# Three of seven block products of an output projection made by seven quarter products each, in an attention kernel on one core

## The chip, the cores and the metric

The kernel runs on one core of a Trainium2 chip. The metric is the device time of one execution in microseconds (us). A core has a tensor engine (PE), a vector engine (DVE), a scalar engine (ACT), GpSimd (POOL) and a sync engine (SP), which here issues all data transfers from one queue, in order. Tiles live in SBUF (128 partitions); PE writes its sums to PSUM banks, which DVE and ACT read[...].

## The reference

Two layers run one after the other on x, of shape (8, 512, 32, 32), float32. Each is a group norm (8 groups in the first, 32 in the second), attention with 8 heads of 64 over the 1024 pixels of an image, an output projection, and the residual added:

```python
qkv = jnp.einsum('oc,bcn->bon', qkv_w, xt) + qkv_b[None, :, None]
...
attn = jnp.einsum('bhdi,bhdj->bhij', q, k) * scale
attn = jax.nn.softmax(attn, axis=-1)
out = jnp.einsum('bhij,bhdj->bhdi', attn, v)
out = out.reshape(B, C_, N)
out = jnp.einsum('oc,bcn->bon', proj_w, out) + proj_b[None, :, None]
return out.reshape(B, C_, H, W) + residual
```

## The kernel before

A *unit* is one image in one layer: 16 units u, 0 to 7 in layer 0 and 8 to 15 in layer 1. The program is written out for all of them, and every engine runs its part in program order. Unit u consists of the products q, k and v (`projections`), then the output projection of the unit before (`project(old, ...)`), then attention with 64 steps. So the projection of unit 3 stands in the middle of unit 4. The last unit's projection (`project_last`) stands at the end and is made in another way.

**Seven block products.** q, k, v and the projection are 512x512 by 512x1024 products. `blocks` makes each of them from halves: with the Strassen-Winograd scheme, four result quarters need seven products of half size in place of eight. The left factors are made once per layer from the weights (`mix_weights`), the right ones per unit (`mix_right`). A product by factor k is four matmuls of 128x128 by 512 columns (L352), and each stands in the profile as two records. `blocks` takes the factors in the order 1, 6, 2, 7, 5, 4, 3, in the PSUM banks bx, by, bz, and calls `done` after each. DVE adds the banks to partial sums p1, u2, u3 (`c11`, `others`).

**Quarter products.** For q and k of every unit but the first, three of the seven (`INNER`, factors 2, 4 and 3) are split again (`last_products`): seven products of 128x128 by 256 columns (L370) in place of four matmuls of 512. Parts that don't go straight into the bank go through two scratch banks `one` and `two`, from which ACT copies them to an SBUF tile `rest`; PE writes `one` again only when the copy is done. Then GpSimd adds two quarters of `rest` (L390, L391) and adds `rest` to the result tiles (`rests`, L470). The right factors are made by GpSimd (`mix_inner`), the left ones once per layer (`mix_inner_left`), which then go by way of DRAM.

**The projection** (`project`) makes all seven in full. DVE adds bias and residual (`plus`, L507) and writes the result into the residual tiles w.res, from which each half tile is stored at once by SP (`store`, L528):

```python
w.evac[h] = nc.vector.tensor_add(
    w.res[o][:, ts(h, FD)], bank[:, i, :], more[:, i, :]
)
store(o, h)
```

`others` is called for result quarters (1,1), (1,0) and (0,1) in this order; (1,0) concerns residual tiles 2 and 3, (0,1) tiles 0 and 1.

**Attention.** At step s PE makes scores s (L603) and, two steps later at first, the product with v (L631); ACT makes the exponential between them (L611) and DVE sums it (L648, L650). The exponentials' tiles p are four buffers of `ppool`, the same that w.res had: the first four exponentials write to the buffers in the order in which these come free. `gate` makes PE wait for what has read a bank. Between two chunks of eight steps, `evacuate` copies a bank to a `tmp` tile of `tmppool` and DVE adds to it. `accpool`, `trpool`, `tpool` hold DVE's sums, transposes and the mixed factors.

**GpSimd's other work.** Its queue also has, in unit 7 ahead of the projection of unit 6, the mixing of layer 1's weights:

```python
if u == B - 1:
    lefts, mixing_w = mix_weights(1, load_weights(1), nc.gpsimd)
    for part in mixing_w:
        part()
```

**Order of small work.** `rest` in the main loop lists work by the running number g of `done` calls: 1 to 7 in q, 8 to 14 in k, 15 to 21 in v. At 17, 19 and 20 DVE makes the right factors of the coming projection (L769).

Of the kernel before, what the change touches and what calls it, by code (L numbers as in the profile page):

```python
# [11 lines left out]
F32 = mybir.dt.float32  # L12
# [6 lines left out]
P = 128  # L19
# [13 lines left out]
def fast_path(ctx, tc, x, qkv_wT, proj_wT, vecs, groups, out, flag):  # L33
# [14 lines left out]
    nc = tc.nc  # L48
    B, C, N = x.shape
# [13 lines left out]
    def pool(name, bufs, **kw):  # L63
# [8 lines left out]
    ppool = pool("ppool", 4)  # L72
    accpool = pool("accpool", 2)
    tpool = pool("tpool", 1)
    tmppool = pool("tmppool", 2)
    trpool = pool("trpool", 2)
    rbpool = pool("rbpool", 1)
    small = pool("small", 2)
# [15 lines left out]
    okay = const.tile([P, 2 * BL], F32, name="okay")  # L94
    asum = const.tile([P, 2 * B * CC], F32, name="asum")

    inner_left = [
        mids.tile([P, 2, len(INNER), 3, P], F32, tag=f"il{l}", name=f"il{l}") for l in range(2)
    ]
# [57 lines left out]
    def mix_right(name, low, high):  # L157


        b11, b12 = low[:, :, :FD], low[:, :, FD:]  # L160
        b21, b22 = high[:, :, :FD], high[:, :, FD:]
        t1, t2, t4 = (
            tpool.tile([P, 2, FD], F32, tag=f"{name[0]}{k}", name=f"{name}_t{k}")
            for k in (1, 2, 4)
        )
        sub = nc.vector.tensor_sub
        parts = (
            partial(sub, t1, b12, b11), partial(sub, t2, b22, t1),
            partial(sub, t4, b21, t2), partial(sub, b12, b22, b12),
        )  # L170
        return {1: b11, 2: b21, 3: b22, 4: t4, 5: t1, 6: t2, 7: b12}, parts

    def mix_inner(u, right):

# [16 lines left out]
    def inner_lefts(k, left, made):  # L191
        a11, a12 = left[:, 0, :P], left[:, 1, :P]
        a21, a22 = left[:, 0, P:], left[:, 1, P:]
        s1, s2, s4 = (made[:, i, :] for i in range(3))
        return {1: a11, 2: a12, 3: s4, 4: a22, 5: s1, 6: s2, 7: a21}

    def mix_inner_left(l, lefts):


        add, sub = nc.gpsimd.tensor_add, nc.gpsimd.tensor_sub  # L200

        def part(n, k):
            t = tpool.tile([P, 2, FD], F32, tag=("o1", "o2", "o4")[n], name=f"l{k}_{l}")
            t = t.rearrange("p a b -> p (a b)")[:, : 6 * P].rearrange("p (i s o) -> p i s o", i=2, s=3)
            for i in range(2):
                left = lefts[i][k]
# [7 lines left out]
                nc.sync.dma_start(inner_left[l][:, i, n], t[:, i])  # L214

        return [partial(part, n, k) for n, k in enumerate(INNER)]

    def load_inner_left(u):

        l, _ = units[u]  # L220
        flat = vpool.tile([P, NT, C], F32, tag="v", name=f"il_{u}").rearrange("p t o -> p (t o)")
        n = len(INNER) * 3 * P
        made = []
        for i in range(2):
            part = flat[:, i * n : (i + 1) * n].rearrange("p (k s o) -> p k s o", s=3, o=P)
            nc.sync.dma_start(part, inner_left[l][:, i])
            made.append({k: part[:, j] for j, k in enumerate(INNER)})
        return made, flat[:, NT * C - 2 * FD :].rearrange("p (a b) -> p a b", a=2)

    def load_proj(l, tag):  # L230
# [100 lines left out]
    class Unit:  # L331
        pass

    def blocks(name, left, right, tokens, c11, others, done, u3, inner=None, rests=None):

        bx, by, bz = apair[0], sbank[0], apair[1]
        sums = []  # L340

        def products(bank, k, start, stop):
            a, b = left[k], right[k]
# [14 lines left out]
        def last_products(bank, k, one, two):  # L358


            if inner is None:
                products(bank, k, False, True)
                return None
            left, right = inner[k]
            one, two = one[:, 0, :FD2], two[:, 0, :FD2]
            tag = ("o1", "o2", "o4")[INNER.index(k)]
            rest = tpool.tile([P, 2, FD], F32, tag=tag, name=f"m{k}_{name}")

            def product(j, dst, start, stop):
                nc.tensor.matmul(  # L370
                    dst, left[j], right[j], start=start, stop=stop, skip_group_check=True
                )
# [8 lines left out]
            nc.scalar.copy(rest[:, 1, FD2:], two)  # L381
            product(4, bank[:, 1, :FD2], False, True)
            product(7, one, False, True)
            nc.scalar.copy(rest[:, 1, :FD2], one)
            return rest

        def add_rest(r, h, rest):
# [37 lines left out]
        others(0, 1, bz, u2)  # L425
        add_rest(0, 1, rest)
        done(sums)

    def projections(w, rest):

# [12 lines left out]
        for sel, bias in (("q", QB), ("k", KB)):  # L443
# [30 lines left out]
            if w.inner:  # L474
# [4 lines left out]
            blocks(f"{sel}_{u}", left, w.right, False, c11, others, done, u3, inner, rests)  # L479
            setattr(w, sel, tiles)  # L480

        w.v = vpool.tile([P, NT, C], F32, tag="v", name=f"v_{u}")
# [16 lines left out]
    def project(w, after):  # L499
# [30 lines left out]
        def c11(bank):  # L530
            for i in range(2):
                cols = w.res[i][:, :FD]
                plus(cols, i, bank[:, i, :], cols)
                store(i, 0)

        def others(r, h, bank, more):
            for i in range(2):
                o = 2 * r + i
                w.evac[h] = nc.vector.tensor_add(  # L539
                    w.res[o][:, ts(h, FD)], bank[:, i, :], more[:, i, :]  # L540
                )
                store(o, h)

        w.evac = [None, None]
        blocks(f"o_{w.u}", w.left, w.right_o, False, c11, others, done, (rbpool, "rb"))

    def project_last(w, rest):

# [24 lines left out]
    def attention(w, at_step, at_end):  # L573
# [6 lines left out]
        n_chunks = CC * NH  # L580
        n_steps = n_chunks * NT
        state = {"exp": [], "p": [], "free": [[], []], "acc": {}}

        def scores(s):
            c, t = divmod(s, NT)
# [30 lines left out]
        def products(s):  # L616
            p = state["p"][s]
            c, t = divmod(s, NT)
            pr, qh = divmod(c, NH)
            banks = abank[2 * (c % 2) : 2 * (c % 2) + 2]  # L620
            before = [state["exp"][s]]
            if t == 0:
                before += state["free"][c % 2]
            if s == 0:
                before += w.last["v"] + w.evac_before
            gate(*before)
            for r in range(2):
                rows = slice(r * H, (r + 1) * H)
                for j in range(2):
                    lo = pr * P + j * D  # L630
                    nc.tensor.matmul(  # L631
                        banks[r][j * H : (j + 1) * H, :],
                        w.v[rows, t, lo : lo + D],
                        p[rows, j, :],
                        start=(t == 0),
                        stop=(t == NT - 1),
                    )
# [14 lines left out]
        def evacuate(c):  # L652
            pr, qh = divmod(c, NH)
            banks = abank[2 * (c % 2) : 2 * (c % 2) + 2]
            tmp = tmppool.tile([P, FD], F32, tag="tmp", name=f"tmp_{u}_{c}")
            i0 = nc.scalar.copy(tmp, banks[0])  # L656
            i1 = nc.vector.tensor_add(w.ao[pr // 2][:, pr % 2, ts(qh, FD)], banks[1], tmp)  # L657
            state["free"][c % 2] = [i0, i1]
# [100 lines left out]
            for h in range(NH):  # L759
                add_bias(CC - 1, h)  # L760

        mixing = []

        def mix(*which):
            if not mixing:
                w.right_o, parts = mix_right(f"o_{u}", *w.ao)
                mixing.extend(parts)
            for i in which:
                mixing[i]()  # L769

        return {
            4: [lambda: reciprocals(CC - 1)], 10: [divide_last],
            17: [partial(mix, 0, 1)], 19: [partial(mix, 2)], 20: [partial(mix, 3)],
        }


    xn = load_xn(0)
# [15 lines left out]
    for u in range(2 * B):  # L793
        w = Unit()
        w.u, w.right, w.lefts, w.inner = u, right, lefts, None
        w.evac_before = []

        rest.setdefault(2, []).extend([mixing[3], mixing[2]])
        if u > 0:
# [3 lines left out]
                part()  # L803
            rest[2].extend(parts[-4:])
        if u == B + 1:
            rest[16] = mixing_o
        projections(w, rest)
        if old is not None:
            old.res = load_res(old.u)
# [10 lines left out]
        if u == B - 1:  # L820
            lefts, mixing_w = mix_weights(1, load_weights(1), nc.gpsimd)
            for part in mixing_w:
                part()
        left_parts = mix_inner_left(units[u + 1][0], lefts) if u in (0, B - 1) else ()

        def stats_of(*which):
            for i in which if nxt is not None else ():
# [324 lines left out]
```

## Time and profile before

| | |
|---|---|
| Three runs | 3311.31, 3311.65, 3310.22 us; median 3311.31 |
| Profiled execution | 3310.82 us, span 3308.9 us from first to last instruction, granted PE clock 1.0 |
| Busy | PE 99%, PE's weight loads 52%, DVE 74%, ACT 46%, POOL 19% |
| PE matmuls by line | attention L631 1098.8 us and L603 1056.9 us plus 50.8 us |
| Projection's block products, L352 on o_t and ao | each group of 120 records 53.9 us |
| Store of a half residual tile, L528 | 256 KB, 2.1 us from issue to landing |

In the profile a row names a line of the kernel, an engine, an operation and the tiles (written <- read). "Busy" is the union of the durations of a group. Matmuls are pipelined, so two that follow each other overlap in the timeline; the distance between their starts tells what one costs. In brackets stands how long the engine was idle before, and what ended that. SPq and ACTq are the queues of the engines. A span can be compared with the runs' times only after the small difference between them.

### The profile page before, as it was taken

What the parts mean: (1) busy time and instruction counts of PE and PEld (TensorE: products, weight loads), DVE (VectorE), ACT (ScalarE), POOL (GpSimd) and SP (SyncE); (2) the same over time, 40 slices, a digit from 0 to 9 for tenths busy, and PEclk for the clock granted to TensorE, in tenths of its full rate; (3) what the DMA queues carried; (4) which work ended last, traced back from release to release, by engine and by line L of the source; (5) the groups of instructions that cost most, each with busy time, mean ns of one, the idle gap of its engine ahead of it and who ended that gap; (6) DMA issues with size and microseconds to landing.
All of it is one profiled execution on the core that took longest, in us unless ns stands there. A gap on an engine that the chain in (4) does not pass through costs nothing.

```text
span 3308.9 us, 53663 instructions
## 1 busy us (share of the span) xinstructions
PE 3281.0 (99%) x21542; PEld 1736.5 (52%) x21542; DVE 2435.9 (74%) x2977; ACT 1525.1 (46%) x1909; POOL 616.7 (19%) x620
## 2 busy tenths in 40 slices
PE   8999999999999999999999999999999999999999
PEld 4445464554645546455464644646456464554633
DVE  4876958769587695867958679586795967859577
ACT  1552726527164361743617436273462734527244
POOL 0231030300304013044220401204021040210400
PEclk9999999999999999999999999999999999999999
DMA  2111020111101112012120111201112011120111
GB/s 78 43 46 71 23 77 27 47 65 36 66 29 51 58 36 77 21 48 96 50 84 27 48 58 36 83 15 47 65 36 77 15 53 58 36 77 15 60 65 47
DMA packets 72906, 169.48 MB, mean 51 GB/s; under 512 B 21456, under 2 KB 23248, under 8 KB 72656
## 3 DMA queue, kind: packets, MB, share of 16 engines
q1 hardware_dynamic: 72656, 166.01, 15.1%
q8 instruction: 174, 2.85, 0.4%
q14 instruction: 76, 0.62, 0.1%
HBM read 127.95 MB, written 36.44 MB: 50 GB/s over the span
## 4 chain that ended last, share of the span: by engine, by line
PE 99%; DVE 1%; DMA 0%; issue 0%; ACT 0%; POOL 0%; SPq 0%; ACTq 0%
PE a L631 26%; PE s L603 25%; PE a L352 20%; PE s L352 16%; PE a L370 4%; PE s L370 4%; PE a L603 1%; PE s L554 0%; PE a L554 0%; DMA xn<-x_dram 0%; DVE x L539 0%; DVE stats L247 0%; PE a L259 0%; ACT p L611 0%; DVE acc L648 0%
## 5 line engine op out<-in xcount | busy, mean ns | idle before, releaser
L611 ACT ACTIVATE p<-s 128x1024 f32<-128x1024 f32 x976 | 996.9, 1023 | 819.5 <-PE s L603 785.2
L631 PE MATMUL a<-p,v 64*64 64x512 f32 x8192 | 1098.8, 589 | 2.3 <-ACT p L611 2.3
L603 PE MATMUL s<-q,k 64*64 64x512 f32 x7808 | 1056.9, 590 | 1.4 <-DVE v L492 1.4
L650 DVE TENSOR_TENSOR acc<-acc,p 128x1024 f32<-128x1024 f32 x768 | 952.2, 1240 | 90.4 <-ACT p L611 42.2
L631 PEld LDWEIGHTS a<-p,v 64*64 64x64 f32 x8192 | 382.1, 131 | 499.6 <-ACT p L611 352.1
L603 PEld LDWEIGHTS s<-q,k 64*64 64x64 f32 x7808 | 380.9, 133 | 442.0 <-issue 439.5
L803 POOL TENSOR_TENSOR r<-xn 128x256 f32<-128x256 f32 x60 | 75.0, 1250 | 1166.7 <-DVE acc L650 1049.4
L279 POOL TENSOR_TENSOR y<-var,half 128x4 f32<-128x4 f32 x16 | 32.2, 2014 | 1052.0 <-DVE var L277 1052.0
L648 DVE TENSOR_TENSOR acc<-p,p 128x1024 f32<-128x1024 f32 x128 | 153.9, 1203 | 12.0 <-ACT p L611 11.9
L663 DVE STREAM_TRANSPOSE tr<-acc 128x1024 f32<-128x1024 f32 x128 | 157.9, 1234 | 0.0
L673 DVE TENSOR_REDUCE red<-tr 128x32 f32<-128x1024 f32 x128 | 153.9, 1202 | 0.6
L657 DVE TENSOR_TENSOR ao<-a,tmp 128x512 f32<-128x512 f32 x128 | 87.9, 687 | 68.2 <-ACT tmp L656 68.1
L352 PE MATMUL a<-xn,w 128*128 128x512 f32 x272 | 125.6, 605 | 4.0 <-DVE xn L307 4.0
L400 ACT COPY p_o<-a 128x1024 f32<-128x1024 f32 x15 | 15.2, 1012 | 244.2 <-PE a L352 244.2
L352 PE MATMUL s<-xn,w 128*128 128x512 f32 x256 | 115.2, 593 | 1.6 <-DVE xn L441 1.6
L352 PE MATMUL a<-w,xn 128*128 128x256 f32 x512 | 115.7, 379 | 0.0
L352 PE MATMUL a<-x_t,s1w 128*128 128x512 f32 x256 | 115.1, 592 | 0.0
L352 PE MATMUL s<-x_t,s2w 128*128 128x512 f32 x256 | 115.1, 592 | 0.0
L470 POOL TENSOR_TENSOR k<-k,m_k 128x512 f32<-128x512 f32 x90 | 112.2, 1268 | 0.0
L470 POOL TENSOR_TENSOR q<-q,m_q 128x512 f32<-128x512 f32 x90 | 112.0, 1265 | 0.0
L352 PE MATMUL a<-ao,wproj_wproj 128*128 128x512 f32 x240 | 107.9, 592 | 0.0
L352 PEld LDWEIGHTS a<-w,xn 128*128 128x128 f32 x512 | 97.3, 190 | 13.7 <-issue 0.5
(195 smaller groups left out, 3795.3 us busy)
## 6 DMA issues: line engine op xcount, KB each, us to landing
rb<-drec SPq DMA_DIRECT2D x128, 256.0 KB, 3.9
xn<-mid SPq DMA_DIRECT2D x36, 512.0 KB, 5.0
il<-il SPq DMA_DIRECT2D x30, 576.0 KB, 4.2
xn<-x_dram SPq DMA_DIRECT2D x32, 512.0 KB, 4.9
x<-x_dram SPq DMA_DIRECT2D x32, 512.0 KB, 3.2
mid<-x SPq DMA_DIRECT2D x64, 256.0 KB, 2.1
x<-mid SPq DMA_DIRECT2D x28, 512.0 KB, 3.5
out_dram<-x SPq DMA_DIRECT2D x56, 256.0 KB, 2.1
```

The lines of the kernel that those rows point to most:

```text
L352: nc.tensor.matmul(dst, at[:, c, ts(i, P)], moving[:, c, :], start=start and c == 0 and not (tokens and i % 2), stop=stop and c == 1, skip ...
L370: nc.tensor.matmul(dst, left[j], right[j], start=start, stop=stop, skip_group_check=True)
L470: w.last[sel].append(nc.gpsimd.tensor_add(cols, cols, rest[:, i, :]))
L603: nc.tensor.matmul(bank[e * H : (e + 1) * H, j, :], w.k[pr][j * H : (j + 1) * H, t * P + e * H : t * P + (e + 1) * H], w.q[pr][j * H : (j ...
L611: exp = nc.scalar.activation(p, bank, AF.Exp, scale=SCALE)
L631: nc.tensor.matmul(banks[r][j * H : (j + 1) * H, :], w.v[rows, t, lo : lo + D], p[rows, j, :], start=(t == 0), stop=(t == NT - 1),)
L648: nc.vector.tensor_add(acc, state["first"], p)
L650: nc.vector.tensor_add(acc, acc, p)
L657: i1 = nc.vector.tensor_add(w.ao[pr // 2][:, pr % 2, ts(qh, FD)], banks[1], tmp)
L663: nc.vector.transpose(tr, state["acc"].pop(c))
L673: nc.vector.tensor_reduce(red[:, :, qh, :], state["tr"].rearrange("p j (f i) -> p j f i", i=BL), AX.X, ALU.add)
L803: part()
```

## The change

In `project`, the products by factors 2, 4 and 3 are made by quarter products, like those of q and k, for all units but 0 and 8 (the first of each layer) and 15 (`project_last`): 13 of 16 units.

- PE makes 3 x 7 quarter products in place of 3 x 4 matmuls of 512 columns; ACT copies four quarters of each to `rest`.
- `rest` of factors 2 and 4 is the one buffer "tmp" of `tmppool`, which has one buffer of two halves in place of two buffers; attention's `tmp` is now a half of it. That of factor 3 is a buffer of `accpool`.
- GpSimd adds the parts to the residual tiles (`rests`), and six of the eight half tiles are stored after that, from there; (1,1) is stored after DVE's addition as before.
- PE's scores of step 1 wait for ACT's last copy (`taken_before`).
- GpSimd makes the right factors (`mix_inner_o`) at 18, 19 and 20, in the buffers of the x factors x2, x1 and x4, after DVE's factors, which are now made at 17, 18 and 19.
- The left factors are made once per layer in attention of units 1 and 9, stored in DRAM, and loaded for each unit by SP: eight of the nine at 15 into a buffer of `trpool`, the ninth at 20 into the spare quarter of the x4 buffer.

Its core:

```diff
-    tmppool = pool("tmppool", 2)
+    tmppool = pool("tmppool", 1)
...
-        t1, t2, t4 = (
-            tpool.tile([P, 2, FD], F32, tag=f"{name[0]}{k}", name=f"{name}_t{k}")
-            for k in (1, 2, 4)
-        )
...
+        factors = {1: b11, 2: b21, 3: b22, 7: b12}
+
+        def part(i):
+            if i == 0:
+                for k, n in ((5, 1), (6, 2), (4, 4)):
+                    factors[k] = tpool.tile([P, 2, FD], F32, tag=f"{name[0]}{n}", name=f"{name}_t{n}")
+            t1, t2, t4 = (factors[k] for k in (5, 6, 4))
+            nc.vector.tensor_sub(
+                *((t1, b12, b11), (t2, b22, t1), (t4, b21, t2), (b12, b22, b12))[i]
+            )
+
+        return factors, [partial(part, i) for i in range(4)]
...
+    def mix_inner_o(u, right, k):
...
+        sub = nc.gpsimd.tensor_sub
+        b = right[k]
+        b11, b12 = b[:, 0, :FD2], b[:, 0, FD2:]
+        b21, b22 = b[:, 1, :FD2], b[:, 1, FD2:]
+        tag = {2: "x2", 3: "x1", 4: "x4"}[k]
+        t = tpool.tile([P, 4, FD2], F32, tag=tag, name=f"ro{k}_{u}")
+        t1, t2, t4 = (t[:, i, :] for i in range(3))
+        sub(t1, b12, b11)
+        sub(t2, b22, t1)
+        sub(b12, b22, b12)
+        sub(t4, b21, t2)
+        return {1: b11, 2: b21, 3: b22, 4: t4, 5: t1, 6: t2, 7: b12}, t[:, 3, :]
...
-            tag = ("o1", "o2", "o4")[INNER.index(k)]
-            rest = tpool.tile([P, 2, FD], F32, tag=tag, name=f"m{k}_{name}")
+            at, tag = rests_in[k]
+            rest = at.tile([P, 2, FD], F32, tag=tag, name=f"m{k}_{name}")
...
-            nc.scalar.copy(rest[:, 1, :FD2], one)
+            taken.append(nc.scalar.copy(rest[:, 1, :FD2], one))
...
+        return taken[-1:]
...
             for i in range(2):
                 cols = w.res[i][:, :FD]
                 plus(cols, i, bank[:, i, :], cols)
-                store(i, 0)
+                if not w.inner_o:
+                    store(i, 0)
...
+                if not w.inner_o or (r, h) == (1, 1):
+                    store(o, h)
+
+        def rests(r, h, rest):
+            for i in range(2):
+                o = 2 * r + i
+                cols = w.res[o][:, ts(h, FD)]
+                nc.gpsimd.tensor_add(cols, cols, rest[:, i, :])
                 store(o, h)
...
-        blocks(f"o_{w.u}", w.left, w.right_o, False, c11, others, done, (rbpool, "rb"))
+        w.taken = blocks(
+            f"o_{w.u}", w.left, w.right_o, False, c11, others, done, (rbpool, "rb"), w.inner_o, rests,
+            {2: (tmppool, "tmp"), 4: (tmppool, "tmp"), 3: (accpool, "acc")},
+        )
...
+        tmps = tmppool.tile([P, 2, FD], F32, tag="tmp", name=f"tmp_{u}")
...
+            elif s == 1:
+                before = before + w.taken_before
...
-                before += w.last["v"] + w.evac_before
+                before += w.last["v"] + w.evac_before + w.taken_before
...
-            tmp = tmppool.tile([P, FD], F32, tag="tmp", name=f"tmp_{u}_{c}")
+            tmp = tmps[:, c % 2, :]
...
+        w.right_o, mixing = mix_right(f"o_{u}", *w.ao)
+        w.inner_o = None
+        parts = {4: [lambda: reciprocals(CC - 1)], 10: [divide_last], 17: mixing[:2], 18: mixing[2:3],
+                 19: mixing[3:]}
+        if u in (0, B):
+            return parts
...
+        w.inner_o = {}
+        l, _ = units[u]
+        src = inner_left_o[l].rearrange("p i k s o -> p (i k s) o")
+        lefts = []
...
+        def load_left():
+            n = 2 * FD // P
+            t = trpool.tile([P, n, P], F32, tag="tr", name=f"lo_{u}")
+            nc.sync.dma_start(t, src[:, :n, :])
+            lefts.extend(t[:, i, :] for i in range(n))
+
+        def mix_inner(k):
+            right, room = mix_inner_o(u, w.right_o, k)
+            if k == INNER[-1]:
+                lefts.append(room[:, :P])
+                nc.sync.dma_start(lefts[-1], src[:, len(lefts) - 1, :])
+            w.inner_o[k] = right
+
+        def finish():
+            for i, k in enumerate(INNER):
+                w.inner_o[k] = (inner_lefts(k, w.left[k], lefts[3 * i : 3 * i + 3]), w.inner_o[k])
+
+        parts[15] = [load_left]
+        parts[18] += [partial(mix_inner, 2)]
+        parts[19] += [partial(mix_inner, 3)]
+        parts[20] = [partial(mix_inner, 4)]
+        w.finish = finish
+        return parts
...
+        left_parts = ()
+        if u in (0, B - 1):
+            left_parts = mix_inner_left(units[u + 1][0], lefts[:2], inner_left)
+        elif u in (1, B + 1):
+            left_parts = mix_inner_left(units[u][0], [left_o], inner_left_o)
...
+            if old.inner_o is not None:
+                old.finish()
...
-            w.evac_before = old.evac
+            w.evac_before, w.taken_before = old.evac, old.taken
```

More of the change, by code (lines that the diff above doesn't have):

```diff
@@ L95, in fast_path @@
     asum = const.tile([P, 2 * B * CC], F32, name="asum")
-    inner_left = [
-        mids.tile([P, 2, len(INNER), 3, P], F32, tag=f"il{l}", name=f"il{l}") for l in range(2)
-    ]
+    inner_left, inner_left_o = (
+        [mids.tile([P, n, len(INNER), 3, P], F32, tag=f"il{l}{n}", name=f"il{l}{n}") for l in range(2)]
+        for n in (2, 1)
+    )
     mid = [mids.tile([C, N], F32, tag=f"mid{b}", name=f"mid{b}") for b in range(B)]
@@ L161, in mix_right @@
         b21, b22 = high[:, :, :FD], high[:, :, FD:]
-        t1, t2, t4 = (
-            tpool.tile([P, 2, FD], F32, tag=f"{name[0]}{k}", name=f"{name}_t{k}")
-            for k in (1, 2, 4)
-        )
[L166 to L171, printed above, removed]
+        factors = {1: b11, 2: b21, 3: b22, 7: b12}
[8 more added lines that the diff above has]
+        return factors, [partial(part, i) for i in range(4)]
     def mix_inner(u, right):
@@ L193, in inner_lefts, with mix_inner_left @@
         a21, a22 = left[:, 0, P:], left[:, 1, P:]
-        s1, s2, s4 = (made[:, i, :] for i in range(3))
+        s1, s2, s4 = made
         return {1: a11, 2: a12, 3: s4, 4: a22, 5: s1, 6: s2, 7: a21}
-    def mix_inner_left(l, lefts):
+    def mix_inner_o(u, right, k):
[11 more added lines that the diff above has]
+        return {1: b11, 2: b21, 3: b22, 4: t4, 5: t1, 6: t2, 7: b12}, t[:, 3, :]
+    def mix_inner_left(l, lefts, dst):
         add, sub = nc.gpsimd.tensor_add, nc.gpsimd.tensor_sub
@@ L204, in part @@
             t = t.rearrange("p a b -> p (a b)")[:, : 6 * P].rearrange("p (i s o) -> p i s o", i=2, s=3)
-            for i in range(2):
-                left = lefts[i][k]
+            for i, left in enumerate(lefts):
+                left = left[k]
                 a11, a12 = left[:, 0, :P], left[:, 1, :P]
@@ L213, in part @@
                 sub(s4, a12, s2)
-                nc.sync.dma_start(inner_left[l][:, i, n], t[:, i])
+                nc.sync.dma_start(dst[l][:, i, n], t[:, i])
         return [partial(part, n, k) for n, k in enumerate(INNER)]
@@ L226, in load_inner_left @@
             nc.sync.dma_start(part, inner_left[l][:, i])
-            made.append({k: part[:, j] for j, k in enumerate(INNER)})
+            made.append({k: [part[:, j, i, :] for i in range(3)] for j, k in enumerate(INNER)})
         return made, flat[:, NT * C - 2 * FD :].rearrange("p (a b) -> p a b", a=2)
@@ L332, in fast_path, with blocks @@
         pass
-    def blocks(name, left, right, tokens, c11, others, done, u3, inner=None, rests=None):
+    def blocks(name, left, right, tokens, c11, others, done, u3, inner=None, rests=None,
+               rests_in=None):
         bx, by, bz = apair[0], sbank[0], apair[1]
-        sums = []
+        sums, taken = [], []
         def products(bank, k, start, stop):
@@ L478, in projections @@
                 }
-            blocks(f"{sel}_{u}", left, w.right, False, c11, others, done, u3, inner, rests)
+            blocks(
+                f"{sel}_{u}", left, w.right, False, c11, others, done, u3, inner, rests,
+                {k: (tpool, tag) for k, tag in zip(INNER, ("o1", "o2", "o4"))},
+            )
             setattr(w, sel, tiles)
@@ L541, in others @@
                 )
+                if not w.inner_o or (r, h) == (1, 1):
[5 more added lines that the diff above has]
+                nc.gpsimd.tensor_add(cols, cols, rest[:, i, :])
                 store(o, h)
         w.evac = [None, None]
-        blocks(f"o_{w.u}", w.left, w.right_o, False, c11, others, done, (rbpool, "rb"))
+        w.taken = blocks(
+            f"o_{w.u}", w.left, w.right_o, False, c11, others, done, (rbpool, "rb"), w.inner_o, rests,
+            {2: (tmppool, "tmp"), 4: (tmppool, "tmp"), 3: (accpool, "acc")},
+        )
     def project_last(w, rest):
@@ L760, in divide_last @@
                 add_bias(CC - 1, h)
[L762 to L774, printed above, removed]
+        w.right_o, mixing = mix_right(f"o_{u}", *w.ao)
[28 more added lines that the diff above has]
+        return parts
     xn = load_xn(0)
@@ L795, in fast_path @@
         w.u, w.right, w.lefts, w.inner = u, right, lefts, None
-        w.evac_before = []
+        w.evac_before, w.taken_before = [], []
         rest.setdefault(2, []).extend([mixing[3], mixing[2]])
@@ L805, in fast_path @@
         if u == B + 1:
-            rest[16] = mixing_o
+            rest.setdefault(16, []).extend(mixing_o)
         projections(w, rest)
@@ L823, in fast_path @@
                 part()
-        left_parts = mix_inner_left(units[u + 1][0], lefts) if u in (0, B - 1) else ()
+        left_parts = ()
[3 more added lines that the diff above has]
+            left_parts = mix_inner_left(units[u][0], [left_o], inner_left_o)
         def stats_of(*which):
```

## The prediction

> **What bounds the kernel now.** I read the page's chain first, then the groups of the tensor engine (PE), then the timeline around one output projection on every engine. The page and the start of the PE timeline:
>
> ```profile
> span 3308.9 us, 53663 instructions
> ...
> PE 3281.0 (99%) x21542; PEld 1736.5 (52%) x21542; DVE 2435.9 (74%) x2977; ACT 1525.1 (46%) x1909; POOL 616.7 (19%) x620
> ...
> PE 99%; DVE 1%; DMA 0%; issue 0%; ACT 0%; POOL 0%; SPq 0%; ACTq 0%
> ```
>
> PE makes 99% of the chain, and only 27.9 us of the span are not PE. So time is saved by giving PE less work, and lost by every gap put into PE's stream; GpSimd (POOL, 19%), ScalarE (ACT) and the queues count only where PE comes to wait for them. The PE timeline, k's last block of unit 4 and then unit 3's projection, whose seven block products I call A to G in program order (factors 1, 6, 2, 7, 5, 4, 3):
>
> ```profile
> 866.15 0.59 PE L370 MATMUL s<-r,s4w 128*128 128x256 f32 x2
> 866.58 3.62 PE L352 MATMUL a<-w,xn 128*128 128x256 f32 x16
> ...
> 907.92 3.60 PE L352 MATMUL s<-o_t,wproj_wproj 128*128 128x512 f32 x8
> 911.36 3.60 PE L352 MATMUL a<-ao,s4w 128*128 128x512 f32 x8
> 914.88 1.95 PE L603 MATMUL s<-q,k 64*64 64x512 f32 x16
> 916.65 1.04 PE L603 MATMUL a<-q,k 64*64 64x512 f32 x8
> 917.51 1.04 PE L631 MATMUL a<-p,v 64*64 64x512 f32 x8
> ...
> 920.94 1.04 PE L631 MATMUL a<-p,v 64*64 64x512 f32 x8
> ```
>
> Starts matter, since shown durations overlap. A block product of the projection starts 911.36 - 907.92 = 3.44 after the one before (3.43 over the six steps from 890.76). A block made by quarter products is already in q and k: k's last went from 863.56 to 866.58, 3.02 us. The projection ends at 911.36 + 3.43 = 914.79 (call this end zero), and attention follows with no gap: scores 0 at 0.09, the first product with v at 2.72, the third at 920.94, which is 6.15.
>
> Next, who could come late. GpSimd on k's last two blocks, then ACT at the start of unit 7's attention:
>
> ```profile
> 863.35 0.73 POOL L390 TENSOR_TENSOR m_k<-m_k 128x256 f32<-128x256 f32 x1 [5.78 <-ACT m_k L381]
> 864.27 0.73 POOL L391 TENSOR_TENSOR m_k<-m_k 128x256 f32<-128x256 f32 x1 [0.20 <-ACT m_k L384]
> 864.96 2.50 POOL L470 TENSOR_TENSOR k<-k,m_k 128x512 f32<-128x512 f32 x2
> 867.43 0.73 POOL L390 TENSOR_TENSOR m_k<-m_k 128x256 f32<-128x256 f32 x1
> 868.24 0.72 POOL L391 TENSOR_TENSOR m_k<-m_k 128x256 f32<-128x256 f32 x1
> 868.92 2.49 POOL L470 TENSOR_TENSOR k<-k,m_k 128x512 f32<-128x512 f32 x2
> ```
>
> ```profile
> 1529.60 1.99 ACT L611 ACTIVATE p<-s 128x1024 f32<-128x1024 f32 x2 [20.62 <-PE s L603]
> 1531.99 1.03 ACT L611 ACTIVATE p<-a 128x1024 f32<-128x1024 f32 x1 [0.40 <-DMA mid<-x]
> 1534.51 1.94 ACT L611 ACTIVATE p<-s 128x1024 f32<-128x1024 f32 x2 [1.49 <-DMA mid<-x]
> ```
>
> Four GpSimd adds take some 4 us for each block, longer than the 3.02 us that PE takes to make one, so two blocks in a row pile up. The second view shows who cares: the first exponentials write into the buffers of the residual tiles, and wait until their store has landed.
>
> **What the Trainium skill says.** "TensorE: Matmul & The Clock Gate", section "Architectural detail", has GpSimd take its instructions strictly in order; the trace has nothing against it. "SBUF — State Buffer", section "SBUF: two separate sides", says that GpSimd and a VectorE (DVE) instruction with two SBUF inputs lock each other out for the whole instruction, with a PSUM input not. The trace agrees: beside the GpSimd adds of L823 the pairs of L507 took 2.74 and 2.86 instead of 1.41, L823 1.71 instead of 1.27, while L539 (from PSUM) kept 1.26. The first page, "What's actually happening", says that PE falls to half clock after about 3.4 us idle and needs about as long to recover. The trace agrees at its start: the first block product took 22.32 - 17.15 = 5.17, against 3.43 later.
>
> **The change part by part**, against the profiled span of 3308.9.
>
> *PE work removed.* Blocks C, F and G become seven quarter products: 3.43 - 3.02 = 0.413 each, three in each of 13 units: 39 x 0.413 = **-16.1 us**. A smaller gain would need a wait inside the blocks. Those of q and k, with the same four ACT copies of 0.37, run without one (0.431 per quarter). The scratch banks are free: sbank[1] lies idle in the projection, DVE has read the others a block earlier. The bound from above is the same 16.1.
>
> *GpSimd makes the right factors*: 12 subtractions of 0.73, up to 1.78 beside DVE (L803 at 818.83): 9 to 21 us. They may start when v's second block is done (873.5), wait for DVE's factors at about 883 and 888, and for the buffer of the x factor until 887.3; I put their end at 893, and C, the first user, starts at 897.6. DVE's four factor subtractions may go from 1.22 to 1.9; v's results have 2 us to spare before PE needs their banks (L492 at 884.05 ends at 885.28, PE takes that bank again at 887.30). Nothing on the path; 0 to 0.3 us a unit, I take 0.
>
> *Left factors by DMA*: 512 KB at step 15 of SP's list and 64 KB at step 20. The small one waits for the x factor's buffer (887.3), and behind it in SP's queue stand the four residual loads, which were issued from 853.9 on. They land some 5 us later, at 892 to 894, and the first reader is L507 at 899.15. 0. The two units that prepare left factors add 12 GpSimd subtractions of 0.46 in attention, where DVE has slack: 0.
>
> *Stores behind GpSimd.* The four half tiles of F and G are stored only when GpSimd has added the parts. What waits: the exponentials. The program hands out the buffers in the order of their last store, so exponentials 0 and 1 take residual tiles 2 and 3 (block F), exponentials 2 and 3 tiles 0 and 1 (G). With k's rhythm, measured from the end of G (866.58 there): GpSimd finishes tile 2 at 864.96 + 1.25 - 866.58 = -0.4, tile 3 at 0.9, tile 0 at 868.92 + 1.25 - 866.58 = 3.6, tile 1 at 4.8. A store lands 2.1 us after issue (page, mid<-x). Exponential 2 thus starts at 5.75 (now 3.1), ends 1.02 later at 6.77, and the third product with v follows at about 6.96 (0.2 from engine to engine, as from PE to ACT). It starts at 6.15 now. Exponential 0 makes the first product late by 0.3, which is part of this; exponential 3 ends by 8.0, in time. PE loses 0.81 a unit and doesn't regain it: 13 x 0.81 = **+10.5 us**. Bounds: 0, if the buffers come free in another way; 2.2 a unit, if DVE slows the three adds up to tile 0's from 1.25 to 1.71 each (0.81 + 3 x 0.46). DVE does PSUM additions and one-input statistics there, so I take 0.81.
>
> *Unit 7, once.* There, ahead of the projection of unit 6, the program puts layer 1's weight mixing onto GpSimd:
>
> ```profile
> 1514.93 1.27 POOL L823 TENSOR_TENSOR s1w<-w 128x512 f32<-128x512 f32 x1 [30.00 <-DMA w<-qkv_wT_dram]
> ...
> 1530.48 1.28 POOL L823 TENSOR_TENSOR s4w<-w,s2w 128x512 f32<-128x512 f32 x1
> ```
>
> Nobody waits for it now. After the change C's four adds stand behind it in GpSimd's queue and finish at 1531.76 + 4.0 = 1535.8. Block F's parts go into the one buffer ("tmp") that C's parts hold until then. ACT's first copy of F waits for it, and PE's fourth quarter product of F, which overwrites what is copied, waits for the copy: 1535.8 + 0.1 + 0.4 + 0.1 = 1536.4. It would be due at 1521.46 - 0.41 + 1.29 = 1522.3. **+14.0 us**. Bounds: 12, if the mixing runs without DVE's contention (12 x 1.23 instead of 16.8); 17, if the later residual loads (2 MB, about 5 us at the 377 to 403 GB/s of this stretch) delay the weights by up to 3 us. After such a pause PE is cold; by the start of the kernel that costs 5.17 - 3.43 = **+1.7 us**.
>
> Sum: -16.1 + 10.5 + 14.0 + 1.7 = +10.1 us: span 3319.0. The three runs have a median of 3311.3, 2.4 above the span shown; so 3321.4.
>
> **Rivals.**
> 1. *The wait for stores is hidden*: unit 7 stands, the start of attention costs nothing. For it: exponential 3 started 6.09 after scores 0 in unit 7 and PE had no gap; against it: PE needs exponential 2, one step earlier. It decides at that place: under 0.54 us a unit the change is within 0.2% (-16.1 + 15.7 + 13 x 0.54 = 6.6), at zero the sum is -0.4, not slower: 3310.9.
> 2. *Unit 7 doesn't stall*, because mixing and sums meet otherwise on GpSimd than I read: -16.1 + 10.5 = -5.6, 3305.7. Against it: order of the program and one buffer.
> 3. *Neither wait*: 3295.2. The change does in the program what it says, 39 blocks.
> 4. *GpSimd is slowed beside DVE, or adds a gap elsewhere*: 2.2 a unit: -16.1 + 28.6 + 15.7 = 28.2, 3339.5.
>
> **How the numbers follow.** A measurement of this kernel can tell about 0.2% (6.6 us) from no change. Chances: my forecast 0.62 (own range 3316 to 3327, from 0.5 to 1.2 a unit and 12 to 17 in unit 7), rival 1 0.15, rival 2 0.08, rival 3 0.05, rival 4 0.10. Slower: forecast and rival 4, 0.72. Same: rival 1 and most of rival 2, 0.20. Faster: rival 3 and the rest of rival 2, 0.08. The range takes in the forecast, rival 1 and the lower half of rival 4, 3309 to 3331.
>
> **What would show it.** Right: 39 x 8 = 312 fewer PE records of full block products and 39 x 14 = 546 more of quarter products, those at the 0.431 of q and k; a PE gap of 0.5 to 1 us at the third product with v in 13 units, with exponential 2 waiting for the store; one PE gap near 14 us in unit 7's block F, the copy released by GpSimd. Wrong: no gap in unit 7, gaps in v's blocks or inside C, F, G, residuals landing after 899 (L507 waiting for DMA), or GpSimd's factors finishing after C's start.

## The result, and the profile after

The changed kernel takes 3327.6 us (median of four runs, 3326.35 to 3329.71). The kernel before, run beside it, takes 3311.5. The ratio is 1.005, with an interval of 1.0032 to 1.0067: 16.1 us slower, beyond the 0.2% that can be told from no change. The forecast was +10.1, to 3321.4; the measured time lies inside the range of 3309 to 3331, and 0.6 above the 3316 to 3327 that the prediction gave for its own theory. The profiled executions differ by 3324.6 - 3308.9 = 15.7 us, and the sums below are made against that.

The head of the page of the changed kernel, and the first line of its chain:

```profile
span 3324.6 us, 54851 instructions
...
PE 3273.6 (98%) x21776; PEld 1847.7 (56%) x21776; DVE 2446.7 (74%) x2977; ACT 1583.0 (48%) x2065; POOL 903.5 (27%) x956
...
PE 93%; POOL 3%; DVE 1%; DMA 1%; issue 1%; ACT 1%; SPq 0%; ACTq 0%; POOLq 0%; DVEq 0%
```

PE is 7 us less busy in a span that is 16 us longer: the change did take work away, and put gaps in. (The 7 are fewer than the 16.1 taken away, since PE's busy records also cover a part of each new gap, and a slow restart.) PE has 21776 - 21542 = 234 records more, which is the 546 - 312 announced. Time that isn't PE's grows from 27.9 to 51.0 us, and the chain now passes through GpSimd (POOL) for 3%. Where the gaps are is said by the list of what PE waited for (total us, times, longest):

```profile
PE a L391 <- ACT m_o L396: 16.3, 1, 16.3
...
PE a L671 <- ACT p L651: 8.5, 18, 2.3
```

One long wait in a quarter product of the projection (L391), and 18 short ones in front of products with v (L671). The longest of the 18, 2.3 us, was there before the change too (`PE a L631 <- ACT p L611: 2.3, 1, 2.3` in that kernel's list); 17 with 6.2 us in total are new. This sum is smaller than what is lost there, since the modelled ends of the records cover a part of each gap; the starts, below, count all of it. The PE timeline around unit 3's projection, as before, and ACT's in the same stretch:

```profile
909.54 0.59 PE L391 MATMUL s<-ao,s4w 128*128 128x256 f32 x2
...
912.13 0.59 PE L391 MATMUL s<-ao,s4w 128*128 128x256 f32 x2
912.65 1.95 PE L643 MATMUL s<-q,k 64*64 64x512 f32 x16
...
915.58 1.09 PE L671 MATMUL a<-p,v 64*64 64x512 f32 x8
...
919.55 1.09 PE L671 MATMUL a<-p,v 64*64 64x512 f32 x8 [0.30 <-ACT p L651]
...
922.05 1.09 PE L671 MATMUL a<-p,v 64*64 64x512 f32 x8 [0.56 <-ACT p L651]
```

```profile
918.38 1.02 ACT L651 ACTIVATE p<-a 128x1024 f32<-128x1024 f32 x1 [1.79 <-DMA mid<-x]
920.89 1.94 ACT L651 ACTIVATE p<-s 128x1024 f32<-128x1024 f32 x2 [1.48 <-DMA mid<-x]
```

Block G runs from 909.54 to 912.56, seven quarters at 0.431, with no gap inside. From its end (end zero) the first product with v starts at 3.02 (2.72 before), the third at 6.99 (6.15 before; 6.96 announced), and the fourth at 9.49. Before, the fourth started at 922.66 - 914.79 = 7.87:

```profile
922.66 1.04 PE L631 MATMUL a<-p,v 64*64 64x512 f32 x8
```

The exponentials wait for the store of the residual tile whose buffer they take (`<-DMA mid<-x` on ACT). The fourth product's wait was not announced. GpSimd in the same stretch:

```profile
910.94 2.50 POOL L575 TENSOR_TENSOR x<-x,m_o 128x512 f32<-128x512 f32 x2
...
914.89 2.50 POOL L575 TENSOR_TENSOR x<-x,m_o 128x512 f32<-128x512 f32 x2
```

The two L575 lines are the pairs of adds of F and G. GpSimd keeps the rhythm that it had on k: tile 0 is done at 914.89 + 1.25 - 912.56 = 3.6, tile 1 at 4.8.

Unit 7: the projection of unit 6 on PE, then ACT, then GpSimd.

```profile
1521.21 0.59 PE L391 MATMUL s<-o_t,ro 128*128 128x256 f32 x2
1538.09 1.22 PE L391 MATMUL a<-ro,lo 128*128 128x256 f32 x2 [16.28 <-ACT m_o L396]
```

```profile
1537.67 0.37 ACT L396 COPY m_o<-a 128x256 f32<-128x256 f32 x1 [23.61 <-POOL x L575]
```

```profile
1516.98 1.27 POOL L886 TENSOR_TENSOR s1w<-w 128x512 f32<-128x512 f32 x1 [12.92 <-DMA w<-qkv_wT_dram]
...
1533.68 0.72 POOL L411 TENSOR_TENSOR m_o<-m_o 128x256 f32<-128x256 f32 x1
```

The reader sees the queue itself: block C's four adds (1533.68 on) stand behind the twelve mixing additions (L886), ACT's copy of F waits for the buffer that they read, and PE's fourth quarter of F waits for the copy.

The whole difference follows from comparing each PE instruction's start with that of the same instruction before, unit by unit:

| term | announced | measured |
|---|---|---|
| three blocks by quarters, 13 units | -16.1 | -16.1 (1.24 in each) |
| start of attention, 13 units | +10.5 | +13.7 |
| unit 7's block F, with the slow restart | +15.7 | +18.5 |
| first unit's start, which varies by up to about 1 us between executions | - | -0.7 |
| sum | +10.1 | +15.5 (span: +15.7) |

### The profile page after: what moved, and what is told of

It is laid out like the page before. It is cut to its first block, busy times and chain, and to the rows that moved or that the text cites. A ratio compares the mean times of both kernels' runs of the same rounds, so it can differ in the third digit from the quotient of the medians.

```text
span 3324.6 us, 54851 instructions
## 1 busy us (share of the span) xinstructions
PE 3273.6 (98%) x21776; PEld 1847.7 (56%) x21776; DVE 2446.7 (74%) x2977; ACT 1583.0 (48%) x2065; POOL 903.5 (27%) x956
## 4 chain that ended last, share of the span: by engine, by line
PE 93%; POOL 3%; DVE 1%; DMA 1%; issue 1%; ACT 1%; SPq 0%; ACTq 0%; POOLq 0%; DVEq 0%
PE a L671 25%; PE s L643 24%; PE a L373 17%; PE s L373 15%; PE a L391 5%; PE s L391 5%; POOL x L575 1%; PE a L643 1%; DMA mid<-x 1%; ACT p L651 0%; DVE acc L690 0%; PE s L591 0%; PE a L591 0%; POOL m_o L411 0%; POOL m_o L412 0%
## 5 line engine op out<-in xcount | busy, mean ns | idle before, releaser
L671 PE MATMUL a<-p,v 64*64 64x512 f32 x8192 | 1120.5, 590 | 9.6 <-ACT p L651 8.5
L643 PE MATMUL s<-q,k 64*64 64x512 f32 x7808 | 1077.3, 590 | 1.4 <-DVE v L517 1.4
L671 PEld LDWEIGHTS a<-p,v 64*64 64x64 f32 x8192 | 403.4, 132 | 492.6 <-ACT p L651 362.4
L643 PEld LDWEIGHTS s<-q,k 64*64 64x64 f32 x7808 | 421.6, 133 | 396.5 <-issue 387.9
L688 DVE TENSOR_TENSOR acc<-p,p 128x1024 f32<-128x1024 f32 x128 | 161.2, 1259 | 29.7 <-ACT p L651 29.7
L298 POOL TENSOR_TENSOR y<-var,half 128x4 f32<-128x4 f32 x16 | 32.2, 2014 | 532.6 <-DVE var L296 532.6
L320 ACT ACTIVATE xn<-xn,shift,scale 128x512 f32<-128x512 f32 x124 | 99.3, 803 | 6.6 <-DVE shift L316 6.6
```

Source lines behind the costliest of these rows:

```text
L320: nc.scalar.activation(cols, cols, AF.Identity, bias=st["shift"][:, c : c + 1], scale=st["scale"][:, c : c + 1],)
L643: nc.tensor.matmul(bank[e * H : (e + 1) * H, j, :], w.k[pr][j * H : (j + 1) * H, t * P + e * H : t * P + (e + 1) * H], w.q[pr][j * H : (j ...
L671: nc.tensor.matmul(banks[r][j * H : (j + 1) * H, :], w.v[rows, t, lo : lo + D], p[rows, j, :], start=(t == 0), stop=(t == NT - 1),)
L688: nc.vector.tensor_add(acc, state["first"], p)
```

## The experiments

Four questions: does the buffer for p carry the whole cost at the start of attention; is it queue order or the one buffer "tmp" that stalls unit 7; what makes the fourth product late in some units; and what is left once the waits are gone. The baselines run beside them have medians of 3311.0 to 3311.2.

**Mixing after the projection.** The additions are issued behind the projection's on GpSimd:

```diff
-            for part in mixing_w:
-                part()
...
+            if u == B - 1:
+                for part in mixing_w:
+                    part()
```

> Unit 7's weight mixing on GpSimd is issued after the projection of unit 6 instead of before it; nothing else changes. My theory (GpSimd's in-order queue makes that projection wait): the 16.3 us PE gap in block F of unit 7 and the cold PE after it go away, 18.5 us, and the mixing then runs beside attention's first chunks, where it may cost 0 to 2 us through DVE's sums: 3327.6 - 18.5 = 3309 to 3311, about as before the change. Rival (the gap comes from the late weights and residual loads on the DMA queue, not from the queue order on GpSimd): the gap stays, 3325 or more.

Measured: 3314.85 us (3312.59 to 3316.57), ratio 1.0011, 1.0002 to 1.0019. The gap in block F is gone, and with it the 18.5 us. The loads were left where they stood, so the rival, late loads, falls. But 5.4 us come back in unit 7's attention, more than the 0 to 2 expected. There DVE, GpSimd and PE show:

```profile
1538.72 11.20 DVE L690 TENSOR_TENSOR acc<-acc,p 128x1024 f32<-128x1024 f32 x5 [1.11 <-ACT p L651]
```

```profile
1539.92 2.27 POOL L903 TENSOR_TENSOR s4w<-w,s2w 128x512 f32<-128x512 f32 x1
```

```profile
1553.84 0.22 PE L278 MATMUL a<-mv,gmat 64*64 64x4 f32 x2 [2.76 <-DVE mv L270]
```

DVE's softmax sums take 2.24 us instead of 1.24, and GpSimd's additions up to 2.27 instead of 1.27, as if each waited for the other's instruction to end. DVE falls behind with the statistics of the next unit's norm, and PE stands 2.76 us in front of the small products that need the mean, and later 2.21 in front of those that need the variance. The stall is confirmed as queue order; the free place for the mixing isn't free.

**Other buffers for the exponentials.** The first three exponentials of each attention take buffers of factors that are no longer in use, not those of residual tiles:

```diff
-            p = ppool.tile([P, 2, FD], F32, tag="p", name=f"p_{u}_{s}")
+            at, tag = (tpool, ("o2", "o1", "o4")[s]) if s < 3 else (ppool, "p")
+            p = at.tile([P, 2, FD], F32, tag=tag, name=f"p_{u}_{s}")
```

> The first three exponentials of each attention write to the buffers o2, o1 and o4, which the projection's factors have left, instead of to those of the residual tiles; the later ones go on as before. My theory (PE waits at the start of attention because exponentials 0, 2 and 3 wait for stores that stand behind GpSimd's adds): the gaps at the first, third and fourth product with v go away in 13 units, 13.7 us by the difference of the two traces: 3327.6 - 13.7 = 3314. Unit 7's gap stays. Rival (scores wait for ACT's last copy, or ACT's copies themselves hold up the exponentials): no more than 2 us is gained, 3326.

Measured: 3313.5 us (3311.48 to 3314.51), ratio 1.0006, 0.9998 to 1.0014: 14.1 us less than the changed kernel. Its PE timeline around the same projection:

```profile
912.13 1.95 PE L643 MATMUL s<-q,k 64*64 64x512 f32 x16
...
914.76 1.04 PE L672 MATMUL a<-p,v 64*64 64x512 f32 x8
...
918.19 1.04 PE L672 MATMUL a<-p,v 64*64 64x512 f32 x8
...
919.91 1.04 PE L672 MATMUL a<-p,v 64*64 64x512 f32 x8
```

and of its list of PE's waits:

```profile
PE a L391 <- ACT m_o L396: 15.7, 1, 15.7
...
PE a L672 <- ACT p L652: 2.3, 1, 2.3
```

The first, third and fourth product with v stand 2.63, 6.06 and 7.78 behind the scores, as before the change (917.51, 920.94 and 922.66 against 914.88). Of the 18 waits for an exponential only the old one is left; the long wait in unit 7 stays. So the whole cost at the start of attention is the exponentials' wait for the stores of those tiles, and these PE gaps are not GpSimd's slowness as such.

**A buffer of its own for block F's parts.** Then ACT's copy needn't wait for C's adds:

```diff
-            {2: (tmppool, "tmp"), 4: (tmppool, "tmp"), 3: (accpool, "acc")},
+            {2: (tmppool, "tmp"), 4: (tpool, "o2"), 3: (accpool, "acc")},
```

> The parts of factor 4 get a buffer of their own (o2, free since block B) instead of sharing one with those of factor 2. Theory A (the queue of GpSimd is the cause, the shared buffer only the place where it shows): in unit 7 block F runs through, but the stores of the residual tiles come as late as GpSimd, so PE waits for exponentials at the start of that attention instead; 3 to 5 us gained at most: 3323. Theory B (the shared buffer is the cause): unit 7's 18.5 us go away: 3309.

Measured: 3323.71 us (3322.47 to 3324.27), ratio 1.0037, 1.0024 to 1.005. Block F runs through, and PE meets the delay in the attention behind it:

```profile
1545.26 1.98 PE L671 MATMUL a<-p,v 64*64 64x512 f32 x8 [12.61 <-ACT p L651]
```

```profile
1544.09 2.13 ACT L651 ACTIVATE p<-s 128x1024 f32<-128x1024 f32 x2 [15.70 <-DMA mid<-x]
```

The exponential waits for a store, the store for GpSimd's adds, the adds for the mixing. The buffer only chose where PE stops; it is the order on GpSimd that costs. Theory B, that the shared buffer is the cause, falls.

**Empty instructions on PE.** In eight of the 13 units the start of attention costs the 0.8 us announced; in units 3, 4, 5, 7 and 8 it costs 0.25 to 0.84 more, since the fourth product with v is late too. In these five the last store landed after 2.96 to 3.31 us, in the others after 2.0. The DMA view of two windows of the changed kernel, in unit 4 (late) and, where no fetch fell, in a later unit (in time):

```profile
q8 instruction: 1, 0.02, 1.6%
...
mid<-x SPq DMA_DIRECT2D x1, 256.0 KB, 3.3
```

```profile
out_dram<-x SPq DMA_DIRECT2D x1, 256.0 KB, 2.0
```

The late window has one packet of 16 KB on the queue of instruction fetches, the other window has no line of that queue. In all five late units such a packet took 0.95 to 1.36 us on one of the 16 DMA engines, and started 0.43 to 0.88 us after the store was issued. Unit 8 has a second reason: its last store took 2.7 us before the change too, with no fetch near, beside the load of layer 1's projection weights that is issued 0.4 us behind it. To shift the fetches, 128 empty instructions are put at the head of PE's stream, with all else unchanged:

```diff
+    for _ in range(128):
+        nc.tensor.nop(nofuse=True)
```

> 128 empty PE instructions at the very start, while PE waits for data anyway; they only shift where PE's instruction stream is fetched. Theory (an instruction fetch of 16 KB on one DMA engine delays the last residual store from 2.0 to 3.0 to 3.3 us, and with it exponential 3): the fourth product's gap leaves units 3, 4, 5, 7 and 8 or turns up in others, wherever a fetch starts 0.4 to 0.9 us after the store's issue; time 3324 to 3328. Rival (stores to the intermediate array of layer 0 are slower in those units): the same five units stay late by 0.3 to 0.8 us.

Measured: one run, 3327.55 us. Landing of the last store, in us:

| unit | changed kernel | with empty instructions | fetch started after the store's issue, with empty instructions |
|---|---|---|---|
| 3, 4, 5 | 2.96, 3.31, 3.20 | 3.27, 2.87, 2.86 | 0.85, 0.46, 0.45 |
| 6 | 2.02 | 3.18 | 0.46 |
| 7 | 3.27 | 2.44 | -0.59 |
| 8 | 3.24 | 2.66 | -1.01 |

Unit 6 became late when a fetch fell into its store, and the last store of units 7 and 8 less late when theirs came ahead of it. There the fetch fell into the store before the last, which landed after 3.08 and 3.17 instead of 1.98 and 2.06, and it is the third product with v, not the fourth, that is late. So the delay is not tied to the unit, and the rival falls. The insertion moved the fetches only in part (units 3 to 5 stayed), but the ten traces of this case can be counted together: in 44 stores of residual half tiles a 16 KB fetch started 0.2 to 1.5 us after the issue, and all landed after 2.8 to 4.3 us. Of the 1028 with no fetch under way, only ten took more than 2.6, all in units 7 and 8 beside loads of layer 1's weights. No run takes a fetch away and changes nothing else, so this is a very close match, short of a proof.

**Both repairs**, the mixing after the projection and the other buffers for p; the edits are the two above.

> The two edits together: weight mixing issued after the projection in unit 7, and the first three exponentials in the free buffers. My theory (two separate waits that add up): 3327.6 - 12.7 - 14.1 = 3301, which is faster than the kernel before by 10 us; what is then missing from the 16.1 us of saved PE work is some 5.4 us in unit 7, where the mixing beside attention slows DVE's sums. Rival (one of them hid a part of the other, or the block products save less than read): 3305 or more.

Measured: 3303.72 us (3302.4 to 3304.62), ratio 0.9978, 0.9969 to 0.9986: 7.3 us faster than the kernel before, between the theory (3301) and its rival (3305). All 13 units keep their 1.24, so nothing was hidden; but unit 7's attention now loses 8.0, where the run with the mixing alone lost 5.4. The trace shows where. PE waits 1.87 for the mean and 4.10 for the variance, against 2.76 and 2.21 there: two tiny instructions of DVE ahead of the variance now fall beside an addition, and take 1.03 and 1.19 us instead of 0.16. And after the 4.10 PE makes two groups at half pace (1.57 and 1.59 from start to start, not 0.86).

**The mixing spread over four chunks of attention**, three additions in each, with the other buffers for p:

```diff
-            for part in mixing_w:
-                part()
...
+            first = 5 if u == B - 1 else 3
+            if t == 0 and first <= c < first + len(left_parts):
+                left_parts[c - first]()
+            if u == B - 1 and 2 <= c < 6 and t in (1, 3, 5):
+                mixing_w[3 * (c - 2) + t // 2]()
```

> As the two edits together, but the twelve mixing additions are issued one by one in attention of unit 7, three to a chunk from chunk 2 to 5, and layer 1's left factors two chunks later. Theory (with the mixing back to back, GpSimd and DVE's sums block each other in SBUF, DVE is late with the next unit's mean and PE waits for it, 2.8 and 2.2 us): spread out, DVE's slack of about 2 us per chunk takes it, 5 us less than the two edits together: 3296, the whole of the 16.1 us. Rival (any addition on GpSimd beside DVE's sums costs PE time): 3300 or more.

Measured: 3302.79 us (3301.47 to 3303.49), ratio 0.9975, 0.9966 to 0.9984. The theory that spreading saves it falls: 8.1 us are lost again. DVE, GpSimd, ACT and PE:

```profile
1554.00 1.21 DVE L308 TENSOR_SCALAR h<-w 128x4 f32<-128x4 f32 x1
1555.24 0.16 DVE L310 TENSOR_TENSOR rstd<-y,h 128x4 f32<-128x4 f32 x1
```

```profile
1546.09 2.06 POOL L298 TENSOR_TENSOR y<-var,half 128x4 f32<-128x4 f32 x1 [19.92 <-DVE var L296]
...
1553.90 1.28 POOL L918 TENSOR_TENSOR s1w<-w 128x512 f32<-128x512 f32 x1
```

```profile
1560.23 1.02 ACT L652 ACTIVATE p<-s 128x1024 f32<-128x1024 f32 x1 [5.64 <-DVE acc L689]
```

```profile
1561.40 1.99 PE L672 MATMUL a<-p,v 64*64 64x512 f32 x8 [4.46 <-ACT p L652]
```

A place in the program is no place in time. GpSimd's queue stands until 1546 for the variance (L298). What is behind it there waits for nothing, so nine of the twelve spread additions run back to back (1548 to 1561). In this stretch DVE has a chain of seven tiny instructions on 4 elements a partition. Six of them take 1.02 to 1.21 us instead of 0.16, each up to the end of an addition (L308 ends at 1555.21, the addition beside it at 1555.18); L310 got in between two. So the chain takes 7.3 us, the sums behind it come late, and exponential and PE with them. After 4.46 us without work PE restarts at half pace (the next group starts 1.73 later, not 0.86).

**Two blocks instead of three.** Factor 3, block G, is made in full again; its half tiles are stored right after DVE:

```diff
...
-            if inner is None:
+            if inner is None or k not in inner:
...
-                if not w.inner_o or (r, h) == (1, 1):
+                if not w.inner_o or (r, h) != (1, 0):
...
-            for i, k in enumerate(INNER):
+            for i, k in ((0, 2), (2, 4)):
...
-        parts[19] += [partial(mix_inner, 3)]
```

> The changed kernel with factor 3 of the projection made in full again: two quarter-product blocks for each of 13 units instead of three, so PE has 13 x 0.41 = 5.4 us more to do. My theory (the last block's adds are what the exponentials of tiles 0 and 1 wait for): their stores then follow DVE at once, the 13.7 us at the start of attention go away almost wholly, and the sum falls: 3327.6 + 5.4 - 13.7 = 3319. Rival (the first of the two adds, tiles 2 and 3, holds up attention just as much): 3328 to 3333.

Measured: 3319.72 us (3318.14 to 3320.91), ratio 1.0027, 1.0017 to 1.0037. The saving falls from 1.24 to 0.82 a unit, the gaps at the start of attention go, and the stall in unit 7 stays (16.7 us). Less of the change is 7.9 us faster than all of it: block G by quarters saved 5.4 and cost the 13.7, so the rival, that the first of the two adds holds up attention just as much, falls.

**The mixing where GpSimd is free.** With the other buffers for p, the weights of q and k for layer 1 are loaded earlier, at step 15 of unit 7's list, and mixed between GpSimd's projection factors and block C's adds; v's four additions go into attention, one in each of four chunks:

```diff
+            rest[15].append(load_early)
+            rest[21] = [mix_early]
...
-            lefts, mixing_w = mix_weights(1, load_weights(1), nc.gpsimd)
-            for part in mixing_w:
-                part()
+            (left_v,), mixing_w = mix_weights(1, load_weights(1, (2,)), nc.gpsimd, 2)
+            lefts = early["lefts"] + [left_v]
...
+            if u == B - 1 and 2 <= c < 6 and t == 3:
+                mixing_w[c - 2]()
```

> Free buffers for the first three exponentials, and the mixing of layer 1's weights moved to where GpSimd is idle: q's and k's weights are loaded during v of unit 7 and mixed right after GpSimd's factors (eight additions, about 10 us, ahead of block C's adds), v's four additions singly in attention, one to a chunk. Theory (the rest that the two earlier edits left, 8 us in unit 7, is DVE being slowed by mixing beside its sums, and GpSimd has about 10 us without work between its factors and block C's adds): unit 7 loses 0 to 2 us, 3303.7 - 7 = 3296 to 3298. Rival (wherever the mixing goes, GpSimd or the transfers make up for it): 3302 or more.

Measured: 3296.82 us (3295.28 to 3299.26), ratio 0.9957, 0.9943 to 0.997: the fastest, 14.3 us ahead of the kernel before and 30.8 of the changed one. Its GpSimd timeline:

```profile
1499.03 1.27 POOL L879 TENSOR_TENSOR s1w<-w 128x512 f32<-128x512 f32 x1
...
1507.84 1.72 POOL L879 TENSOR_TENSOR s4w<-w,s2w 128x512 f32<-128x512 f32 x1
1509.52 1.17 POOL L411 TENSOR_TENSOR m_o<-m_o 128x256 f32<-128x256 f32 x1
```

The eight additions fill GpSimd's gap before C's parts, PE runs through the projection, and v's four cost 1.6 us in attention, all as the theory had it (3296 to 3298). Of the 16.1 us that PE saves, 14.3 arrive.

## Why the prediction was right, and where its sizes were off

*PE work removed* held to the tenth: 39 blocks, 1.24 a unit, no wait inside the blocks.

*GpSimd makes the right factors* and *Left factors by DMA* cost nothing in any unit. In unit 4 the factors were done at 890.2 (893 announced), and C started at 896.6.

*Stores behind GpSimd* had the right mechanism, shown by the run with other buffers, and the right size in the units without a fetch: 0.8 against 0.81. The term of the sum that was mis-sized is 13 x 0.81 = 10.5, measured 13.7. It took every store to land after 2.1 us, the median of the page, and so let exponential 3 end "by 8.0, in time". In five units the last store took 3.0 to 3.3, and the fourth product was late as well. That exponential has about half a us to spare (8.0 + 0.2 against the 6.99 + 1.72 at which its product is due), and a chain with so little in hand should not be run through a median: late landings were to be seen before the change too, where the last store of unit 7 took 4.0, and that of unit 8 took 2.7.

*Unit 7, once* had the right mechanism, confirmed from both sides: the gap goes when the mixing is issued later, and moves when the buffer is exchanged. It was put at +14.0 and the pause measured 16.3; the additions began 13.4 us after the projection did, not 10.6. The prediction had named the cause in its bound of 17 (the residual loads, issued later, delay the weights by up to 3 us) and took the other end. Its own working had those loads moved close to the start of the projection, where the weights are loaded too; the value for the sum should have held that. The first weights were issued at 1506.3 in both traces, and landed at 1516.9 instead of 1514.8, behind 2 MB of residuals that had been issued from 1500.8 on. The slow restart, +1.7 announced, is what is left of the 18.5, some 2 us, with four quarter products at half pace.

Rival 1 fell at the third product, rival 2 at the gap in block F, rival 3 at both. Rival 4 had its effect in the wrong place: DVE doesn't slow the adds of F and G. Where mixing and DVE's sums were brought together, in the experiments, mutual blocking did cost 5 to 8 us.

## What to carry to other kernels

Work taken off the busiest engine counts only as long as the helper that takes the rest isn't in the way of something the busy engine needs soon: look what a helper's result frees (here a store, then a buffer, then an exponential), and what already stands in the helper's queue. If a wait is only for a buffer, another buffer costs an edit of two lines and gave 14 us back; if it is for a place in a queue, another buffer only moves it. Put helper work where the helper is idle in time, not where the program has room.

## What the runs showed that was not expected

- A store is late when an instruction fetch falls into it: each of the 44 stores of 256 KB in whose flight a 16 KB packet started, 0.2 to 1.5 us after the issue, landed after 2.8 to 4.3 us instead of some 2.0.
- Tiny DVE instructions suffer most beside GpSimd: 128x4 took 1.02 to 1.21 us beside back-to-back additions, six times out of seven, and 0.16 alone. The Trainium skill, "SBUF — State Buffer", section "SBUF: two separate sides", has the pair locked for the whole instruction, and these numbers agree. L308, an operation with a scalar and one SBUF tensor, was held up as well; the page also names DVE's 2-port modes as taking the lock, and no run here shows whether that is the reason.
